# Convolutional self-attention on one core: weights loaded by GpSimd, dummy transposes at the start, the first k loads and the first l and d at other steps, the last group in two blocks and stored by SyncE

## The chip, the cores and the metric

The kernel runs on one core of a Trainium2 chip. The metric is the device time of one execution in microseconds (us), as a median of runs. The engines of the core run side by side, each through its own list of instructions in order, and wait for one another by semaphores: TensorE (PE in the profile, with its weight loads as PEld), VectorE (DVE), ScalarE (ACT), GpSimd (POOL) and SyncE (SP). DMAs are issued from the lists of SP, ACT and POOL and run on 16 DMA engines that they share.

## The reference

For each of four images, with x of 64 x 64 positions and 256 channels:

```python
q = jnp.einsum('bwhc,cd->bwhd', x, Wq) + bq       # 128 channels
k = jnp.einsum('bwhc,cd->bwhd', x, Wk) + bk       # 128 channels
v = jnp.einsum('bwhc,cd->bwhd', x, Wv) + bv       # 256 channels
pq = q.reshape(B, -1, N)                          # N = 4096
pk = k.reshape(B, -1, N)
pv = v.reshape(B, -1, N)
energy = jnp.einsum('bcn,bcm->bnm', pq, pk)
attention = jax.nn.softmax(energy, axis=-1)
out = jnp.einsum('bcm,bnm->bcn', pv, attention)
return gamma * out.reshape(B, W, H, C) + x
```

All of it is float32. The reshape cuts the memory of an image into rows of 4096, whatever the channel a number came from.

## The kernel before, in words

**Numbers in parts.** PE is fed with a rounded 32-bit type. Each factor of the two large products is therefore split into a head and remainders (`halved`, line 244, for q and k; `project_v`, line 262, for v; `upper` and `halves`, lines 320 and 325, for the exponentials), and three products of parts take the place of one.

**The projection of an image.** It has 16 steps (`NI`), i = 0 to 15. A step transposes one block of x (256 KB, loaded by SP, line 82) on PE (line 123), ACT evicts it (129), PE multiplies it by the q and k weights (136), and DVE adds the biases (145). POOL stores q as it is (257, two DMAs), ACT and DVE split k (247, 249), and POOL stores the three parts of k (260). PE makes the values of the step before (157); ACT adds the bias and rounds (166, 267) and DVE makes the two remainders (270). q and k pass through DRAM, in the tiles `qd` and `kf`, because they are read back in another order.

**The attention of an image.** It has 16 groups of 256 rows (`NG`), each of 8 units (`NU`): 128 units, u = 0 to 127. A unit works on four blocks of 128 columns. POOL reads k (`load_k`, 287, 768 KB), SP reads q once a group (`load_q`, 276), and ACT and DVE split it (`halve_q`). `energy` makes the scores in two halves (303) and ACT the exponentials x and y (307). DVE joins them (`join`, 317), ACT makes the head h (`upper`, 322), DVE the remainders l and d (`halves`, 328 and 331). `attend` (351) multiplies h, l and d by the values into the accumulators `a0`, `a1` and `bb`, for two blocks j of 128 rows. One more column of the values holds ones, so `a0` and `a1` also sum the exponentials.

**The end of a group.** ACT copies `bb` (361). `whole` saves the sums (368) and adds `a0` and `a1` (371). `finish`, in pieces over later units, takes the reciprocal times gamma (378, 379), scales (381), transposes (389), adds x (393) and stores through POOL (394).

**Order.** Everything in the block of line 192 runs in the order in which it is written: each engine's list is the order of the calls. The stretch of an image around the change is

```python
for i in range(1, NI):
    ...
    pr.transposed(i + 1)
    begin(b, i)            # first loads, scores, join and upper of the image
    project_qk(b, i)
    project_v(b, i - 1)
halves(b, 0)
project_v(b, NI - 1)
for u in range(STEPS):
    ...                    # energy(u + 3), join(u + 2), upper(u + 2), halves(u + 1), attend(u)
```

`begin` (398) loads the first q at step 8 and splits it at step 9, loads the k of units 0, 1 and 2 at steps 8, 9 and 10, makes the scores of units 0, 1 and 2 at steps 10 to 15, and joins units 0 and 1 at steps 12 and 14. Outside the block, before line 191 and after line 468, the framework places the instructions. POOL builds the unit matrix `ident` for the transposes (86).

**Buffers.** The k tiles, x and h of a unit have three buffers each, y, l and d two, as have the banks of the scores and the tiles of raw q and of split k. So x of unit 3 needs d of unit 0 done, which is the last reader of x of unit 0.

**The guard.** The fast path leaves out the subtraction of the maximum in the softmax. At the end the sums are compared with two bounds (474 to 477), the result is spread over partitions by a product (480) and cast to a flag `again` (481). Every engine reads the flag and branches over a general path, which does not run here (488).

Of the kernel before, what the change touches and what calls it, by code (L numbers as in the profile page):

```python
# [20 lines left out]
def kernel(  # L21
# [67 lines left out]
    wqk_sb = const.tile([P, KC, 2 * C2], F32, name="wqk_sb")  # L89
    nc.scalar.dma_start(wqk_sb[:, :, :C2], wq.rearrange("(k p) d -> p k d", p=P))  # L90
    nc.scalar.dma_start(wqk_sb[:, :, C2:], wk.rearrange("(k p) d -> p k d", p=P))
    wv_sb = const.tile([P, KC, C], F32, name="wv_sb")
    nc.scalar.dma_start(wv_sb, wv.rearrange("(k p) e -> p k e", p=P))
    bqk_sb = const.tile([P, 2 * C2], F32, name="bqk_sb")
    nc.scalar.dma_start(bqk_sb[:, :C2], bq.partition_broadcast(P))
    nc.scalar.dma_start(bqk_sb[:, C2:], bk.partition_broadcast(P))
    bv_sb = const.tile([P, KC], F32, name="bv_sb")
    for eh in range(KC):
        nc.scalar.dma_start(bv_sb[:, eh : eh + 1], bv[eh * P : (eh + 1) * P].unsqueeze(1))
    gam = const.tile([P, 1], F32, name="gam")  # L100
    nc.scalar.dma_start(gam, gamma.partition_broadcast(P))

    class Projection:

# [78 lines left out]
    UPPER = 1.0 - 2.0**-13  # L183

    again = const.tile([P, 1], I32, name="again")

    zall = const.tile([P, B * NG, NJ], F32, name="zall")
    bv4_sb = const.tile([P, KC], F32, name="bv4_sb")
    nc.scalar.mul(bv4_sb, bv_sb, 1.0 / E)

    with ExitStack() as fast:
        fast.enter_context(tc.manual_schedule())
# [12 lines left out]
        vl = qkv.tile([P, NM, C + 2], F32R, tag="vl", name="vl")  # L205
        vd = qkv.tile([P, NM, C], F32R, tag="vd", name="vd")
        for t in (vh, vl):
            nc.vector.tensor_copy(t[:, :, C:], ones[:, : 2 * NM].rearrange("p (m t) -> p m t", t=2))

        images, qd, kf, units, loads, now = [], {}, {}, {}, {}, {}  # L210

# [124 lines left out]
        def attend(b, u, j):  # L336
            g, t = divmod(u, NU)
            if t == j == 0:
                now["acc"] = [
                    ps_o.tile([P, C + 2], F32, tag=f"a{j}", name=f"a{j}_{b}_{g}")  # L340
                    for j in range(NJ)
                ]
                now["bb"] = ps_o.tile([P, NJ, C], F32, tag="bb", name=f"bb_{b}_{g}")
            h, l, d = units[b, u]
            a, bb = now["acc"][j], now["bb"]
            n = slice(j * P, (j + 1) * P)
            for out_, left, right in ((a, h, vh), (a, l, vl), (bb[:, j, :], d, vd)):
                for i in range(4):
                    m = 2 * t + i // 2 + NI * (i % 2)

                    nc.tensor.matmul(  # L351
                        out_,
                        left[:, i, n],
                        right[:, m, :],
                        start=(t == i == 0 and (left is h or left is d and j == 0)),
                        stop=(t == NU - 1 and i == 3 and left is not h),
                        skip_group_check=True,
                    )
            if t == NU - 1 and j == NJ - 1:
                now["o"] = work.tile([P, NJ, C], F32, tag="o", name=f"o_{b}_{g}")  # L360
                nc.scalar.copy(now["o"], bb)

        def whole(b, g):

            o = now["o"]
            for j in range(NJ):
                a = now["acc"][j]
                nc.vector.tensor_copy(zall[:, b * NG + g, j : j + 1], a[:, C : C + 1])
            for j in range(NJ):
                a = now["acc"][j]  # L370
                nc.vector.scalar_tensor_tensor(
# [2 lines left out]

        def finish(b, g, o, xr):
            yield
            r = work.tile([P, NJ], F32, tag="r", name=f"r_{b}_{g}")
            nc.vector.reciprocal(r, zall[:, b * NG + g, :])
            nc.vector.tensor_tensor(r, r, gam.to_broadcast([P, NJ]), ALU.mult)  # L379
            for j in range(NJ):  # L380
                nc.scalar.activation(  # L381
                    o[:, j, :], o[:, j, :], AF.Identity, scale=r[:, j : j + 1]
# [10 lines left out]
            nc.vector.tensor_tensor(xr, xr, tp, ALU.add)  # L393
            nc.gpsimd.dma_start(ov[b, g], xr)

        def begin(b, i):

            if i == 8:
                load_q(b, 0)
            if i == 9:  # L400
                halve_q(b, 0)
            if 8 <= i <= 10:
                load_k(b, i - 8)
            if i >= 10:
                energy(b, (i - 10) // 2, i % 2)
            if i in (12, 14):
# [6 lines left out]
        for b in range(B):  # L413
# [6 lines left out]
            for i in range(1, NI):  # L420
# [3 lines left out]
                    pr.transposed(i + 1)  # L424
                begin(b, i)
                project_qk(b, i)
                project_v(b, i - 1)
                proceed()
            halves(b, 0)
            project_v(b, NI - 1)  # L430
            for u in range(STEPS):
                g, t = divmod(u, NU)
# [24 lines left out]
                    halve_q(b, ahead // NU + 1)  # L457
                for j in range(NJ):
                    attend(b, u, j)
                if t == NU - 1:  # L460
                    whole(b, g)
                    start(finish(b, g, now["o"], loads.pop((b, "x", g))))
                proceed()
# [2 lines left out]
                project_qk(b + 1, 0)  # L466
            while active:
                proceed()


    zs = const.tile([P, 1], F32, name="zs")
    zf = zall.rearrange("p n j -> p (n j)")
    ok = const.tile([P, B * NG * NJ], F32, name="ok")
    nc.vector.tensor_scalar(ok, zf, Z_LOW, None, ALU.is_ge)
    nc.vector.scalar_tensor_tensor(ok, zf, Z_HIGH, ok, ALU.is_le, ALU.mult)
    nc.vector.tensor_reduce(zs, ok, AX.X, ALU.min)
    nc.vector.tensor_scalar(zs, zs, 0.5, None, ALU.is_lt)
    with tc.tile_pool(name="ps_z", bufs=1, space=PSUM) as ps_z:
        zp = ps_z.tile([P, 1], F32, name="zp")
        nc.tensor.matmul(zp, ones, zs, start=True, stop=True)  # L480
        nc.vector.tensor_copy(again, zp)

    NB = 512
    NG = N // NB
# [132 lines left out]
```

## Time and profile before

| | |
|---|---|
| time, median of 3 runs | 2518.38 us (2517.4 to 2519.71) |
| the profiled execution's own time | 2520.6 us |
| its span | 2518.5 us |
| mean granted PE clock | 0.998 |
| PE busy | 2486.5 us, 99% |
| DVE busy | 2103.0 us, 84% |
| ACT busy | 1806.3 us, 72% |
| POOL busy | 425.3 us, 17% |
| k loads (POOL), 768 KB each | 512, median 4.8 us from issue to landing |
| x loads (SP), 256 KB each | 128, median 3.4 us |
| kf stores (POOL), 384 KB each | 64, median 3.5 us |
| output stores (POOL), 256 KB each | 64, median 2.5 us |

The span is the profiled execution from its first to its last instruction. A row of a timeline begins with the start in the span and the duration; then come the engine, the line of the kernel, the operation, what it writes <- what it reads, shapes, and xN for N instructions merged. In square brackets stands how long the engine was idle before, and behind the arrow what ended that. An engine name with a q, as ACTq, is the engine's issuing side. An end of a PE row is modelled; products that follow one another closely overlap in it.

### The profile page before, as it was taken

The page shows a single profiled execution, that of the slowest core. Times are in us where ns is not written, and L with a number is a line of the kernel's source. Part 1 is how long each engine was busy: PE and PEld are TensorE (multiplying, and loading weights), DVE is VectorE, ACT ScalarE, POOL GpSimd, SP SyncE. Part 2 cuts the span into 40 slices and gives each one's busy share as a digit, 9 for nine tenths or more (in the row PEclk, how much of TensorE's full clock was granted, in tenths as well). Part 3 has the DMA queues.
Part 4 walks back from the last instruction along what each step waited for, and adds up shares of the span by engine and source line. Part 5 has one row for each costly group of instructions (what it writes and reads, how often), then busy time and mean ns, then how long its engine had stood idle before and what let it go on. Part 6 is the DMA issues. An engine that isn't in the chain of part 4 may idle for free.

```text
span 2518.5 us, 49987 instructions
## 1 busy us (share of the span) xinstructions
PE 2486.5 (99%) x19970; PEld 2440.1 (97%) x19970; DVE 2103.0 (84%) x2440; ACT 1806.3 (72%) x3138; POOL 425.3 (17%) x774
## 2 busy tenths in 40 slices
PE   8999999999999999999999999999999999999998
PEld 7999999999899999999989999999998999999998
DVE  5888888888688888888868888888886888888887
ACT  5777777777677777777667777777766777777775
POOL 3211111111411111111041111111114111111110
PEclk9999999999999999999999999999999999999999
DMA  6666666665766666666476666666647666666663
GB/s 220 204 207 206 199 200 194 211 196 156 230 214 190 209 202 201 206 192 203 139 236 210 196 200 208 198 205 197 192 144 243 209 207 192 204 200 206 199 196 101
DMA packets 137967, 498.92 MB, mean 198 GB/s; under 512 B 15872, under 2 KB 57856, under 8 KB 137728
## 3 DMA queue, kind: packets, MB, share of 16 engines
q0 software_dynamic: 92160, 453.03, 57.0%
q1 hardware_dynamic: 44032, 41.96, 5.5%
q8 instruction: 160, 2.62, 0.4%
q10 hardware_dynamic: 1536, 0.66, 0.1%
q14 instruction: 79, 0.65, 0.1%
HBM read 445.25 MB, written 50.33 MB: 197 GB/s over the span
## 4 chain that ended last, share of the span: by engine, by line
PE 91%; issue 3%; ACT 3%; DVE 2%; DMA 1%; POOL 0%; POOLq 0%; ACTq 0%; DVEq 0%
PE a L351 38%; PE bb L351 19%; PE sa L303 18%; PE sb L303 10%; PE qk L136 2%; PE v L157 2%; PE ot L389 1%; ACT v L166 1%; DMA k<-kf 1%; ACT vh L267 1%; DVE qks L145 1%; PE xt L123 0%; ACT f L247 0%; DVE vd L270 0%; DVE x L317 0%
## 5 line engine op out<-in xcount | busy, mean ns | idle before, releaser
L307 ACT ACTIVATE x<-sa 128x512 f32<-128x512 f32 x1024 | 608.8, 595 | 431.3 <-PE sa L303 422.3
L317 DVE TENSOR_TENSOR x<-x,y 128x1024 f32<-128x1024 f32 x512 | 625.1, 1221 | 165.6 <-ACT y L307 165.6
L303 PE MATMUL sa<-q,k 128*128 128x256 f32 x4096 | 744.8, 280 | 8.8 <-DMA k<-kf 4.8
L351 PE MATMUL a<-vh,h 128*128 128x258 f32 x4096 | 666.8, 285 | 0.0
L351 PE MATMUL a<-vl,l 128*128 128x258 f32 x4096 | 659.5, 283 | 1.7 <-DVE l L328 1.7
L351 PE MATMUL bb<-vd,d 128*128 128x256 f32 x4096 | 650.7, 281 | 1.8 <-DVE d L331 1.8
L303 PEld LDWEIGHTS sa<-q,k 128*128 128x128 f32 x4096 | 622.9, 188 | 10.8 <-ACT x L307 5.0
L328 DVE TENSOR_TENSOR l<-x,h 128x1024 fp32r<-128x1024 f32 x512 | 623.2, 1217 | 0.0
L331 DVE SCALAR_TENSOR_TENSOR d<-h,x 128x1024 fp32r<-128x1024 f32 x512 | 623.1, 1217 | 0.0
L307 ACT ACTIVATE y<-sb 128x512 f32<-128x512 f32 x1024 | 612.9, 599 | 0.0
L303 PE MATMUL sb<-q,k 128*128 128x256 f32 x2048 | 576.3, 281 | 0.0
L351 PEld LDWEIGHTS a<-vl,l 128*128 128x128 f32 x4096 | 563.0, 189 | 2.6 <-DVE l L328 2.6
L322 ACT ACTIVATE h<-x 128x1024 fp32r<-128x1024 f32 x512 | 543.3, 1061 | 29.1 <-DVE x L317 29.1
L351 PEld LDWEIGHTS a<-vh,h 128*128 128x128 f32 x4096 | 560.6, 190 | 1.1
L351 PEld LDWEIGHTS bb<-vd,d 128*128 128x128 f32 x4096 | 556.4, 188 | 2.6 <-issue 2.0
L287 POOL DMA_DIRECT2D k<-kf x512 | 283.6, 554 | 1487.3 <-PE sb L303 1470.5
L303 PEld LDWEIGHTS sb<-q,k 128*128 128x128 f32 x2048 | 384.5, 188 | 8.9 <-ACT y L307 1.0
L136 PE MATMUL qk<-wqk_sb,xts 128*128 128x256 f32 x512 | 124.5, 387 | 3.5 <-ACT xts L129 3.5
L157 PE MATMUL v<-xts,wv_sb 128*128 128x256 f32 x512 | 120.3, 379 | 0.0
L381 ACT ACTIVATE o<-o,r 128x256 f32<-128x256 f32 x128 | 58.3, 503 | 73.9 <-DVE r L379 73.9
L157 PEld LDWEIGHTS v<-xts,wv_sb 128*128 128x128 f32 x512 | 97.4, 190 | 13.3
L136 PEld LDWEIGHTS qk<-wqk_sb,xts 128*128 128x128 f32 x512 | 94.5, 194 | 14.7 <-ACT xts L129 3.9
(41 smaller groups left out, 876.2 us busy)
## 6 DMA issues: line engine op xcount, KB each, us to landing
k<-kf POOLq DMA_DIRECT2D x512, 768.0 KB, 4.8
x<-in_x_dram SPq DMA_DIRECT2D x128, 256.0 KB, 3.4
kf<-f POOLq DMA_DIRECT2D x64, 384.0 KB, 3.5
out_dram<-x POOLq DMA_DIRECT2D x64, 256.0 KB, 2.5
qd<-qks POOLq DMA_DIRECT2D x128, 64.0 KB, 2.2
qr<-qd SPq DMA_DIRECT2D x64, 128.0 KB, 3.1
wv_sb<-in_L_conv_Wv_dram ACTq DMA_DIRECT2D x1, 256.0 KB, 4.3
wqk_sb<-in_L_conv_Wq_dram ACTq DMA_DIRECT2D x1, 128.0 KB, 2.1
```

The source lines that it names most:

```text
L136: nc.tensor.matmul(qk[:, s, :], self.xt[i][:, k, s, :], wqk_sb[:, k, :], start=(k == 0), stop=(k == KC - 1),)
L145: nc.vector.tensor_tensor(dst, qk[:, :, o : o + w], bqk_sb[:, o : o + w].unsqueeze(1).to_broadcast([P, 2, w]), ALU.add,)
L157: nc.tensor.matmul(vp[:, eh, :], wv_sb[:, k, eh * P : (eh + 1) * P], self.xt[i][:, k].rearrange("p s a -> p (s a)"), start=(k == 0), stop= ...
L287: nc.gpsimd.dma_start(t.rearrange("p (i s) f d -> p i s (f d)", s=2), kf[b, u % NU])
L303: nc.tensor.matmul(to[:, i], kt[:, 2 * k + i, f, :], q[:, :, f, :], start=first, stop=last)
L307: nc.scalar.activation(to[:, 2 * k : 2 * k + 2, :], sp.rearrange("p i j d -> p i (j d)"), AF.Exp, scale=scale,)
L317: nc.vector.tensor_tensor(x, x, y, ALU.mult)
L322: nc.scalar.activation(h, units[b, u], AF.Identity, scale=UPPER)
L328: nc.vector.tensor_tensor(l, x, h.bitcast(F32), ALU.subtract)
L331: nc.vector.scalar_tensor_tensor(d, h.bitcast(F32), 1.0 + E, x, ALU.mult, ALU.subtract)
L351: nc.tensor.matmul(out_, left[:, i, n], right[:, m, :], start=(t == i == 0 and (left is h or left is d and j == 0)), stop=(t == NU - 1 and ...
L381: nc.scalar.activation(o[:, j, :], o[:, j, :], AF.Identity, scale=r[:, j : j + 1])
```

## The change

1. **Weights and biases.** The two biases, Wv, bv and gamma are loaded by DMAs from POOL's list; only Wq and Wk stay in ACT's. The product of bv and 1/E (line 189) moves from ACT to POOL. The columns of ones in the values (208) are copied by ACT and no more by DVE.
2. **Dummy transposes.** Before the block PE transposes `ident` twelve times into a tile that nothing reads.
3. **Steps of the projection.** The first q load moves from step 8 to step 5, the first k loads from steps 8, 9 and 10 to steps 4, 6 and 8. The first l and d (`halves(b, 0)`) move ahead of the values of step 14, made in the last pass of the loop.
4. **The last group** of the last image has a path of its own, `finish_last`, with the guard spread over it: block 0 and block 1 are each scaled by ACT straight from `bb`, added to by DVE from the accumulators, transposed and added to x, and SP stores the group. The other groups are left as they are.

```diff
     wqk_sb = const.tile([P, KC, 2 * C2], F32, name="wqk_sb")
     nc.scalar.dma_start(wqk_sb[:, :, :C2], wq.rearrange("(k p) d -> p k d", p=P))
     nc.scalar.dma_start(wqk_sb[:, :, C2:], wk.rearrange("(k p) d -> p k d", p=P))
+    bqk_sb = const.tile([P, 2 * C2], F32, name="bqk_sb")
+    nc.gpsimd.dma_start(bqk_sb[:, :C2], bq.partition_broadcast(P))
+    nc.gpsimd.dma_start(bqk_sb[:, C2:], bk.partition_broadcast(P))
     wv_sb = const.tile([P, KC, C], F32, name="wv_sb")
-    nc.scalar.dma_start(wv_sb, wv.rearrange("(k p) e -> p k e", p=P))
-    bqk_sb = const.tile([P, 2 * C2], F32, name="bqk_sb")
-    nc.scalar.dma_start(bqk_sb[:, :C2], bq.partition_broadcast(P))
-    nc.scalar.dma_start(bqk_sb[:, C2:], bk.partition_broadcast(P))
+    nc.gpsimd.dma_start(wv_sb, wv.rearrange("(k p) e -> p k e", p=P))
...
-        nc.scalar.dma_start(bv_sb[:, eh : eh + 1], bv[eh * P : (eh + 1) * P].unsqueeze(1))
+        nc.gpsimd.dma_start(bv_sb[:, eh : eh + 1], bv[eh * P : (eh + 1) * P].unsqueeze(1))
...
-    nc.scalar.dma_start(gam, gamma.partition_broadcast(P))
+    nc.gpsimd.dma_start(gam, gamma.partition_broadcast(P))
...
-    nc.scalar.mul(bv4_sb, bv_sb, 1.0 / E)
+    nc.gpsimd.tensor_scalar(bv4_sb, bv_sb, 1.0 / E, None, ALU.mult)
+    with tc.tile_pool(name="ps_w", bufs=1, space=PSUM) as ps_w:
+        wp = ps_w.tile([P, P], F32, name="wp")
+        for _ in range(12):
+            nc.tensor.transpose(wp, ident, ident)
...
-            nc.vector.tensor_copy(t[:, :, C:], ones[:, : 2 * NM].rearrange("p (m t) -> p m t", t=2))
+            nc.scalar.copy(t[:, :, C:], ones[:, : 2 * NM].rearrange("p (m t) -> p m t", t=2))
...
-            if t == NU - 1 and j == NJ - 1:
+            if t == NU - 1 and j == NJ - 1 and (b, g) != (B - 1, NG - 1):
                 now["o"] = work.tile([P, NJ, C], F32, tag="o", name=f"o_{b}_{g}")
                 nc.scalar.copy(now["o"], bb)
...
+        def guard():
+            z = zall.rearrange("p n j -> p (n j)")
+            nc.vector.tensor_scalar(ok, z, Z_LOW, None, ALU.is_ge)
+            nc.vector.scalar_tensor_tensor(ok, z, Z_HIGH, ok, ALU.is_le, ALU.mult)
+            yield
+            nc.vector.tensor_reduce(zs, ok, AX.X, ALU.min)
+            nc.vector.tensor_scalar(zs, zs, 0.5, None, ALU.is_lt)
+            zp = ps_s.tile([P, 1], F32, tag="b", name="zp")
+            nc.tensor.matmul(zp, ones, zs, start=True, stop=True)
+            yield
+            nc.vector.tensor_copy(again, zp)
+            yield
+            yield
+
+        def finish_last(b, g, xr):
+            sums(b, g)
+            r = factors(b, g)
+            check = guard()
+            ra = work.tile([P, NJ], F32, tag="ra", name="ra", bufs=1)
+            nc.vector.tensor_scalar(ra, r, 1.0 + E, None, ALU.mult)
+            o = work.tile([P, NJ, C], F32, tag="o", name=f"o_{b}_{g}")
+            tps = []
+            for j in range(NJ):
+                next(check)
+                nc.scalar.activation(
+                    o[:, j, :], now["bb"][:, j, :], AF.Identity, scale=r[:, j : j + 1]
+                )
+                nc.vector.scalar_tensor_tensor(
+                    o[:, j, :], now["acc"][j][:, :C], ra[:, j : j + 1], o[:, j, :], ALU.mult, ALU.add
+                )
+                tp = (ps_t, ps_s)[j].tile([P, 2, P], F32, tag="ta"[j], name=f"ot_{b}_{g}_{j}")
+                for s in range(2):
+                    nc.tensor.transpose(tp[:, s, :], o[:, j, s * P : (s + 1) * P], ident)
+                tps.append(tp)
+            for j in range(NJ):
+                next(check)
+                n = slice(j * P, (j + 1) * P)
+                nc.vector.tensor_tensor(xr[:, :, n], xr[:, :, n], tps[j], ALU.add)
+            nc.sync.dma_start(ov[b, g], xr)
+
         def begin(b, i):
-            if i == 8:
+            if i == 5:
                 load_q(b, 0)
             if i == 9:
                 halve_q(b, 0)
-            if 8 <= i <= 10:
-                load_k(b, i - 8)
+            if i in (4, 6, 8):
+                load_k(b, i // 2 - 2)
...
                 project_qk(b, i)
+                if i == NI - 1:
+                    halves(b, 0)
                 project_v(b, i - 1)
                 proceed()
-            halves(b, 0)
             project_v(b, NI - 1)
...
-                if t == NU - 1:
+                if (b, u) == (B - 1, STEPS - 1):
+                    finish_last(b, g, loads.pop((b, "x", g)))
+                elif t == NU - 1:
                     whole(b, g)
```

`sums` and `factors` are the saving of the sums and the reciprocal times gamma, cut out of `whole` and `finish` as they were. The guard's lines after the block (471 to 481) are gone.

## The prediction

> **What bounds the kernel now.** I read the page first, then the chain of waits, and then the timeline around every place where TensorE (PE) stood still. The page settles the scale: PE works for almost the whole span, so only its few pauses, and what lies before its first and after its last product, can be won.
>
> ```profile
> span 2518.5 us, 49987 instructions
> PE 2486.5 (99%) x19970; PEld 2440.1 (97%) x19970; DVE 2103.0 (84%) x2440; ACT 1806.3 (72%) x3138; POOL 425.3 (17%) x774
> ```
>
> 2518.5 - 2486.5 leaves 32 us of idle PE, and some busy PE time is slow. There are four places.
>
> The head. In the timeline of the first microseconds (start, duration, engine) PE has transposed two blocks of x by about 6.5 us and then waits, because ACT, which must evict them, waits at line 189 for the last of its own weight transfers and then loads its table:
>
> ```profile
> 4.33 2.19 PE L123 MATMUL xt<-ident,x 128*128 128x128 f32 x8 [4.33 <-DMA x<-in_x_dram]
> 8.02 1.28 ACT L189 ACT_TABLE_LOAD   x1 [8.02 <-DMA gam<-in_L_conv_gamma_dram]
> 9.43 1.05 ACT L129 COPY xts<-xt 128x512 f32<-128x512 f32 x2
> 10.05 3.78 PE L136 MATMUL qk<-wqk_sb,xts 128*128 128x256 f32 x8 [3.52 <-ACT xts L129]
> 14.44 1.89 PE L136 MATMUL qk<-wqk_sb,xts 128*128 128x256 f32 x8
> ```
>
> The last two lines are the same work: 3.78 us on the slow clock, 1.89 us on the full one.
>
> The first scores of an image (step 10). PE waits for k, in image 2 so long that the clock drops again. PE's timeline, then two rows of the stretch view (length, busy PE, PEld, DVE, ACT, POOL, granted clock, DMA):
>
> ```profile
> 1294.44 0.60 PE L123 MATMUL xt<-ident,x 128*128 128x128 f32 x4
> 1297.11 0.47 PE L303 MATMUL sa<-q,k 128*128 128x256 f32 x2 [2.07 <-DMA k<-kf]
> 1297.96 3.50 PE L136 MATMUL qk<-wqk_sb,xts 128*128 128x256 f32 x8
> 1298.00:1302.00 4.00, 4.00 (x13) 3.24 (x13) 0.52 (x2) 1.07 (x2) 0.04 (x1) 0.60 1.05 354
> 1924.00:1928.00 4.00, 4.00 (x23) 3.53 (x22) 1.53 (x4) 1.92 (x5) 1.11 (x3) 1.00 1.10 401
> ```
>
> The first attend of an image. DVE makes l and d of unit 0 behind the values of step 14; ACT's next exp waits for d, the next h for join(2):
>
> ```profile
> 78.87 0.69 DVE L270 SCALAR_TENSOR_TENSOR vl<-vh,v 128x512 fp32r<-128x512 f32 x1 [0.72 <-ACT vh L267]
> 81.36 0.75 PE L351 MATMUL a<-vl,l 128*128 128x258 f32 x4 [0.43 <-DVE l L328]
> 82.53 0.60 ACT L307 ACTIVATE x<-sa 128x512 f32<-128x512 f32 x1 [1.96 <-DVE d L331]
> 84.81 1.06 ACT L322 ACTIVATE h<-x 128x1024 fp32r<-128x1024 f32 x1 [1.19 <-DVE x L317]
> 86.41 0.50 PE L303 MATMUL sa<-q,k 128*128 128x256 f32 x2 [1.00 <-ACT x L307]
> ```
>
> The tail. PE's last product ends at 2506.20; the rest is a chain of small steps, POOL's store and the closing instructions (the last line is one line of the view by source, durations in ns):
>
> ```profile
> 2506.24 0.59 ACT L361 COPY o<-bb 128x512 f32<-128x512 f32 x1 [6.87 <-PE bb L351]
> 2508.05 0.91 ACT L381 ACTIVATE o<-o,r 128x256 f32<-128x256 f32 x2 [1.22 <-DVE r L379]
> 2509.60 0.69 DVE L393 TENSOR_TENSOR x<-x,ot 128x512 f32<-128x512 f32 x1 [1.64 <-PE ot L389]
> 2510.58 0.70 POOL L394 DMA_DIRECT2D out_dram<-x  x1 [26.11 <-DVE x L393]
> L613 POOLq DRAIN  x3: 45/107/6353, 2511.3 to 2518.2; - x3
> ```
>
> The store lands at 2513.82, SP is through its waits at 2514.44, but POOL's 6.35 us drain ends only at 2517.65, and 0.8 us of barriers follow.
>
> **What the Trainium skill says.** "TensorE: Matmul & The Clock Gate", section "What's actually happening": PE's clock is halved until a free-running window of 3413 ns has been busy, and again after an idle one. The trace agrees: at 1297.80 the clock halves for 3.41 us, and from its rise at 14.39 to there are 376 such windows. The 2.07 us wait of image 2 lay wholly in one window; the 1.99 us of image 3 were split by a boundary, and the clock held. The same page, "Part 4: PE-mode transpose", says that transposes do not count as busy PE for this. The trace does not decide: 1.8 us of transposes in the window from 4.15 to 7.56 did not raise the clock, but they filled only half of it. "DMA: Bandwidth & Descriptors", "Specifications": first byte about 1 us from POOL's path, 0.6 us from SP's. POOL's last store shows 1.27 us (2510.58 to 2511.85). "Runtime: NRT & Kernel Launch", "Instruction fetch mechanics": a taken branch outside the fetched pages stalls for a fetch. SP stood 2.55 us after its branch at 2508.43.
>
> **The change part by part.**
>
> Head. ACT keeps two DMA issues, ending at 1.70; the table load of 1.28 us and two small copies (0.32 and 0.19 us on DVE before) end by about 3.6, covered by the wait for x (4.19). The first eviction then waits only for the transposes (done by 5.42) and ends at 5.45 + 0.57 = 6.02; PE leaves the second pair of transposes at 6.31 (5.41 + 4 x 0.21 and the last one's tail). qk starts near 6.35 instead of 10.05: **3.7 us**. wqk landed at 4.55 and stays on ACT. POOL issues six transfers after its mask at 1.31, 0.70 + 5 x 0.54 us as its qd issues take, until about 4.7. The biases should land near 5.5, when qk's end at 8 wants them; wv near 7.5 (before: 6.06), wanted after 8 + 0.4 + 1.7 = 10; bv and gamma near 7.5, then 0.2 us for bv4 on POOL, behind which only the first qd store queues, ready after 8.7. If a transfer came 2 us late it would cost its excess over these 2 us margins.
>
> Clock. Twelve transposes at the slow spacing 0.213 us fill 1.4 to 4.0. Before, the slow clock lasted 4.34 us past 10.05, half of it lost: 2.17 us. If transposes count, almost all of that is won; if not, the wait for a busy window only starts at 6.35 and nothing is. Bounds -1.2 (a bad phase of the window) and +2.2; I take **1.1**.
>
> k. The load of unit 0 moves from step 8 to 4, of unit 1 from 9 to 6, of unit 2 from 10 to 8. From step 10's transposes to the first attend the images take 31.25, 30.30, 34.28 and 32.52 us. Image 1 did not wait, so the others lose 0.95, 3.98 and 2.22: **7.15 us**, of which 1.76 is image 2's slow clock. On POOL a load now stands ahead of the stores of steps 4, 6 and 8, and must wait for the kf stores of units 0, 1, 2. The nearest pair is two steps (7.8 us) apart, a store lands in 3.5. A load occupies POOL for 0.55 us. The 768 KB also run beside x loads (3.4 us to landing, asked for two steps, 7.8 us, ahead). The 128 KB q load moves from 8 to 5 on SP, behind an x load and ahead of one; its qd stores are four steps old. Both are hidden by these margins.
>
> l and d. After the second f (78.15) DVE would do l, d, then four value instructions, and join(2) as before. It saves the gap of 0.72 us and a little: l at 78.08, each large one 1.136 and each small one 0.60 apart, gives join(2) at 78.08 + 2 x 1.136 + 4 x 0.60 = 82.75 instead of 83.56. PE no longer waits for l and d (0.43 + 0.48), but then waits longer for ACT: h of unit 2 follows join(2), x of unit 3 follows h, and the bank follows x. So the gain is not 0.9 + 1.0, but what join(2) gains: 0.8 an image, **3.2 us**. Late next is DVE itself, with the values of steps 14 and 15, first read in units 6 and 7.
>
> Tail. From 2506.20: reciprocal, two small products and the first two guard instructions keep DVE until 2507.07; ACT scales block 0 by 2506.85; DVE adds (0.41) to 2507.51; two transposes to 2508.05. DVE does the guard's reduction and compare, then block 1 at 2508.04 to 2508.45; its transposes end at 2509.0; the copy of the flag (0.14) and two additions of 0.4 end at 2509.48. SP issues the store at 2509.55, 1.03 before POOL did. Then SP still has to issue (0.6), read the flag (0.5), branch with its fetch (2.6) and pass its waits (1.4): done at about 2514.65, with barriers 2515.45. The landing, 3.4 us as the x loads, is inside that. POOL has had nothing to drain since 2484; if its drain is then short, SP ends the kernel: 2518.47 - 2515.45 = **3.0 us**. If it keeps its 6.35 us from about 2509.3, the end is 2516.5: 1.9 us.
>
> Sum: 3.7 + 1.1 + 7.15 + 3.2 + 3.0 = 18.1 us, against the profiled execution's 2520.6 (span 2518.5): 2502.5. The median, 2518.38, lies 2.2 below that execution, and as the window is free-running the 1.76 us of image 2 need not be in it. I take about 17 us off the median: **2501.5 us**.
>
> **The rivals.**
> *Transposes warm nothing and POOL's drain stays.* The page on the clock speaks for the first, nothing for or against the second. 17 - 1.1 - 1.1 leaves 14.8: 2503.6 us. 0.20.
> *The wait moves from k to x.* The k load took 8.3 us in image 2; 768 KB among x loads may make x late. Against it: x has 4.4 us to spare, and step 8 already had such a load beside x. It takes the 7.15 (5.4 where the clock held): about 2507.5 us. 0.10.
> *The new order is not the order that runs, or the weights arrive late.* Outside the hand-ordered block instructions can be placed elsewhere: the guard of before runs ahead of L371. If POOL's transfers land some 4 us later and k gains nothing, some 4 us remain: 2514.5, not to be told from no change (0.2%, 5 us, is about what this measurement can tell). 0.04.
> *Slower: POOL is held by the early k loads.* If a load waits for its kf store to land, the stores queued behind it are late, f's two buffers fill, and ACT and PE stop. At 3.5 us for each of 12 loads that is 42 us, 25 after the gains: 2543 us. It turns the sign from 17 / 12 = 1.4 us a load. The 7.8 us distance speaks against it. 0.03.
>
> **How the numbers follow.** The forecast has 0.63, with 2499 to 2503.5 as its own range. The clock's bounds, the two drains and a half-failed l and d reach 2497 and 2505.5; the x rival reaches 2508. 2497 to 2508 leaves out the last two cases and some edges. Faster 0.93, same 0.04, slower 0.03.
>
> **What would show it.** The first qk near 6.4 us, its eight products 1.9 us long if the clock is up; no PE wait for k in any image, and none of the slow clock; join(2) 0.8 us earlier after the last projection, with PE's wait for ACT's x grown to 1.8 us in place of those for l and d; a short POOL drain and SP last. It is wrong if PE waits at step 10 or for x, if the first value product waits for wv, or if the drain stays at 6 us.

## The result, and the profile after

The changed kernel takes 2520.06 us (median of 6, 2517.64 to 2522.64), the kernel before 2519.62 us in the same rounds (median of 6, 2517.4 to 2521.11): ratio 1.0002, 95% interval 0.9989 to 1.0015. The forecast was 2501.5, its range 2497 to 2508. It is wrong, and the range with it.

The profiled execution took 2518.42 us with a span of 2516.5. The head of the page of the changed kernel:

```profile
span 2516.5 us, 50017 instructions
PE 2497.4 (99%) x19982; PEld 2455.1 (98%) x19982; DVE 2102.5 (84%) x2440; ACT 1806.1 (72%) x3138; POOL 424.6 (17%) x780
```

The span has shrunk by 2.0 us, but PE's busy time has grown by 10.9, from 2486.5 to 2497.4, with 12 instructions more (the head's transposes). So PE stands still 13 us less, and works 11 us longer. The shorter waits were forecast; the longer work was not. PE's largest waits before, from the view of waits of PE (total, times, longest, us):

```profile
PE sa L303 <- DMA k<-kf: 4.8, 3, 2.1
PE xt L123 <- DMA x<-in_x_dram: 4.3, 1, 4.3
PE sa L303 <- ACT x L307: 4.0, 4, 1.1
```

and after:

```profile
PE sa L311 <- ACT x L315: 6.0, 4, 1.6
PE wp L197 <- POOL ident masks.py:199: 2.4, 1, 2.4
PE ot L446 <- DVE o L441: 1.3, 1, 1.3
PE sa L311 <- DVE q L257: 0.3, 1, 0.3
PE xt L123 <- DMA x<-in_x_dram: 0.2, 1, 0.2
```

The waits for k (4.8), for ACT's xts (3.5), for l and d (1.7 and 1.8) and for x (4.3) are gone or nearly so. The one for ACT's x has grown from 1.0 us to 1.3 to 1.6 each time; the working had said that it would grow, to 1.8. A short wait for DVE's q is new. The head, in the timeline of the changed kernel (start, duration, engine):

```profile
2.05 0.32 POOL masks.py:199 TENSOR_SCALAR_AFFINE_SELECT ident<-ident 128x128 f32<-128x128 f32 x1
2.42 2.82 PE L197 MATMUL wp<-ident 128*128 128x128 f32 x12 [2.42 <-POOL ident masks.py:199]
5.30 1.12 PE L123 MATMUL xt<-ident,x 128*128 128x128 f32 x4
6.64 1.12 PE L123 MATMUL xt<-ident,x 128*128 128x128 f32 x4 [0.22 <-DMA x<-in_x_dram]
7.55 2.29 PE L136 MATMUL qk<-wqk_sb,xts 128*128 128x256 f32 x8
10.11 1.89 PE L136 MATMUL qk<-wqk_sb,xts 128*128 128x256 f32 x8
```

The first qk starts at 7.55 in place of 10.05. POOL's first bias load ran ahead of its mask, so the identity was ready a microsecond late, and the twelve transposes held the first x back from 4.33 to 5.30.

The end, in the timeline, with two lines of the view by source (durations in ns):

```profile
2506.17 0.84 ACT L438 ACTIVATE o<-bb,r 128x256 f32<-128x256 f32 x2 [7.09 <-DVE r L380]
2508.16 0.75 DVE L451 TENSOR_TENSOR x<-x,ot 128x256 f32<-128x256 f32 x2
2508.93 0.60 SPq L452 DMA_DIRECT2D out_dram<-x  x1
L661 POOLq DRAIN  x3: 46/107/6683, 2509.0 to 2516.3; - x3
L661 SPq DRAIN  x3: 7/7/13, 2514.5 to 2516.0; - x3
```

The store leaves 1.65 us earlier (1.39, counted from PE's last product), and SP is through at 2514.5; but POOL's drain lasts 6.68 us, no less than before, and ends last.

What takes all of this back is seen in the groups of the page. The scores before:

```profile
L303 PE MATMUL sa<-q,k 128*128 128x256 f32 x4096 | 744.8, 280 | 8.8 <-DMA k<-kf 4.8
L303 PE MATMUL sb<-q,k 128*128 128x256 f32 x2048 | 576.3, 281 | 0.0
```

and after:

```profile
L311 PE MATMUL sa<-q,k 128*128 128x256 f32 x4096 | 759.2, 282 | 6.3 <-ACT x L315 6.0
L311 PE MATMUL sb<-q,k 128*128 128x256 f32 x2048 | 580.4, 283 | 0.0
```

The two groups overlap in time; together the same 4096 and 2048 products keep PE busy 831.8 us in place of 816.9, 14.9 us longer. The attends (L351, now L359) are 2 us shorter together, qk 3.0, and the twelve new transposes add 2.8. The waits before the scores come to 6.3 us, 2.5 less than before. Close up, one half unit of the timeline before (image 1, the scores after the attend of unit 45; start, duration):

```profile
903.29 0.39 PE L303 MATMUL sa<-q,k 128*128 128x256 f32 x2
903.52 0.28 PE L303 MATMUL sb<-q,k 128*128 128x256 f32 x1
903.64 0.39 PE L303 MATMUL sa<-q,k 128*128 128x256 f32 x2
903.86 0.28 PE L303 MATMUL sb<-q,k 128*128 128x256 f32 x1
903.98 0.39 PE L303 MATMUL sa<-q,k 128*128 128x256 f32 x2
```

and after:

```profile
901.73 0.40 PE L311 MATMUL sa<-q,k 128*128 128x256 f32 x2
901.97 0.28 PE L311 MATMUL sb<-q,k 128*128 128x256 f32 x1
902.09 0.40 PE L311 MATMUL sa<-q,k 128*128 128x256 f32 x2
902.32 0.28 PE L311 MATMUL sb<-q,k 128*128 128x256 f32 x1
902.44 0.40 PE L311 MATMUL sa<-q,k 128*128 128x256 f32 x2
```

Six products take 0.69 us before and 0.71 after. In the unrounded starts they are 113 to 114 ns apart before; after, the distances go 117, 120, 116, 115, 119, 116, 120, 117, 115, 118. The whole group of eight units around them, in the stretch view (length, busy PE, PEld, DVE, ACT, POOL, granted clock, DMA), before:

```profile
878.40:913.16 34.76, 34.76 (x294) 34.61 (x293) 30.17 (x34) 25.86 (x44) 5.03 (x9) 1.00 0.65 201
```

and after:

```profile
876.77:911.75 34.98, 34.98 (x294) 34.85 (x293) 30.18 (x34) 25.91 (x44) 4.96 (x9) 1.00 0.65 201
```

PE is busy throughout, at the full clock in both, and takes 0.22 us longer. The balance between the two profiled executions, from the starts of PE's records:

| stretch | before | after | difference | forecast |
|---|---|---|---|---|
| start to image 0's first score | 50.34 | 45.06 | -5.28 | -5.75 |
| first input product to first score, images 1 to 3 | 119.23 | 114.69 | -4.54 | -6.20 |
| first score to first attend of unit 2, four images | 167.32 | 163.62 | -3.70 | -3.2 |
| from there to the image's last product, four images | 2168.48 | 2181.75 | **+13.27** | 0 |
| last product to the end of the span | 12.27 | 10.59 | -1.68 | -3.0 |
| sum | | | -1.93 | -18.15 |

In the third row 1.67 us of the 3.70 are the slow clock window of image 2 before, which the forecast counts with k. Set there, k gained 6.21 us against this one execution, and l and d 2.03.

### The profile page after: what moved, and what is told of

Its sections match the earlier page's. It is cut to its first block, busy times and chain, and to the rows that moved or that the text cites. A ratio compares the mean times of both kernels' runs of the same rounds, so it can differ in the third digit from the quotient of the medians.

```text
span 2516.5 us, 50017 instructions
## 1 busy us (share of the span) xinstructions
PE 2497.4 (99%) x19982; PEld 2455.1 (98%) x19982; DVE 2102.5 (84%) x2440; ACT 1806.1 (72%) x3138; POOL 424.6 (17%) x780
## 4 chain that ended last, share of the span: by engine, by line
## 5 line engine op out<-in xcount | busy, mean ns | idle before, releaser
L311 PE MATMUL sa<-q,k 128*128 128x256 f32 x4096 | 759.2, 282 | 6.3 <-ACT x L315 6.0
L359 PE MATMUL a<-vh,h 128*128 128x258 f32 x4096 | 662.4, 284 | 0.0
L359 PE MATMUL a<-vl,l 128*128 128x258 f32 x4096 | 660.3, 283 | 0.0
L359 PE MATMUL bb<-vd,d 128*128 128x256 f32 x4096 | 651.9, 281 | 0.0
L359 PEld LDWEIGHTS a<-vl,l 128*128 128x128 f32 x4096 | 563.8, 189 | 0.0
L359 PEld LDWEIGHTS a<-vh,h 128*128 128x128 f32 x4096 | 561.5, 189 | 0.0
L359 PEld LDWEIGHTS bb<-vd,d 128*128 128x128 f32 x4096 | 557.6, 189 | 0.0
```

The costliest lines, as they stand in the source:

```text
L311: nc.tensor.matmul(to[:, i], kt[:, 2 * k + i, f, :], q[:, :, f, :], start=first, stop=last)
L359: nc.tensor.matmul(out_, left[:, i, n], right[:, m, :], start=(t == i == 0 and (left is h or left is d and j == 0)), stop=(t == NU - 1 and ...
```

## The experiments

Run n has the label that begins with e and n.

**What could make the same products slower.** Two theories. *Place*: the only new tile in the pool `work` is `ra`, two numbers per partition for the last group's factors. The pool lays out its tiles in the order in which their tags first appear, in steps of 32 bytes. Counted so from the sizes in the code, the tiles that the loop uses keep their places in both kernels, except the two that come after `ra`: `f` and `k` lie 32 bytes further on. k, the stationary operand of the scores (the one that PE holds), lies at 96 bytes modulo 128 of each partition before and at 0 after. q, which streams past it, lies at 32 in both. *Order*: the moved steps change which transfers and evictions run beside the scores all through an image.

Run 1 is the changed kernel with `ra` in r's buffers, which puts k back:

```diff
-            ra = work.tile([P, NJ], F32, tag="ra", name="ra", bufs=1)
+            ra = work.tile([P, NJ], F32, tag="r", name="ra")
```

> The changed kernel, with ra taken from the two buffers of r, so that the tiles of split k (and of f) keep their old addresses (k at 96 modulo 128 instead of 0). Place theory: the attention is slow because these tiles moved by 32 bytes; a group of eight units goes back from 34.99 to about 34.77 us, the products of the scores in units 3 to 7 of a group to 113.3 ns, and the whole to about 13 us below the changed kernel, some 2506 us. Order theory: the earlier l, d and loads set ACT and DVE into another rhythm against PE; nothing changes, about 2519 us.

Run 2 is the kernel before with nothing but a pad ahead of f and k, in the last group (f and k 32 bytes on):

```diff
+            if (b, g) == (B - 1, NG - 1):
+                pad = work.tile([P, NJ], F32, tag="pad", name="pad", bufs=1)
+                nc.gpsimd.memset(pad, 0.0)
```

> The kernel before, with one more tile of 32 bytes at the end of the work pool (set to zero once by POOL in the last group), so that k and f move by 32 bytes as in the changed kernel and nothing else does. Place theory: a group takes 34.99 us, the whole about 13 us more than before, some 2532 us. Order theory: same as before, 34.77 us a group.

Run 3 is the changed kernel with `bufs=2` for `ra`: k another 32 bytes on.

> The changed kernel with two buffers for ra, so that k and f move by another 32 bytes (k at 32 modulo 128). Place theory: if what counts is the place modulo 64 bytes, as fast as with the old addresses, some 2506 us; if it is modulo 128, anything. Order theory: as the changed kernel, about 2519 us.

Run 4 is the kernel before with the moved steps alone:

```diff
-            if i == 8:
+            if i == 5:
                 load_q(b, 0)
...
-            if 8 <= i <= 10:
-                load_k(b, i - 8)
+            if i in (4, 6, 8):
+                load_k(b, i // 2 - 2)
...
+                if i == NI - 1:
+                    halves(b, 0)
                 project_v(b, i - 1)
...
-            halves(b, 0)
             project_v(b, NI - 1)
```

> The kernel before with only the moved steps (first q load at step 5, k loads at 4, 6 and 8, first l and d before the values of step 14); addresses as before. Place theory: the gain that was forecast for these two parts, 7.15 + 3.2 us by the profile and at least 8.5 in a run whose clock held in image 2, so some 2509 us, with 34.77 us a group. Order theory: the loss of some 13 us in the attention comes with it, some 2522 us, with 34.99 us a group.

| run | median us | ratio, 95% interval | eight units, us |
|---|---|---|---|
| 1, ra in r's buffers | 2508.31 | 0.9944, 0.993 to 0.9957 | 34.77 |
| 2, before with k at 0 | 2534.93 | 1.0055, 1.0041 to 1.0069 | 34.97 |
| 3, changed with k at 32 | 2525.97 | 1.002, 1.0013 to 1.0027 | 35.06 |
| 4, moved steps alone | 2513.53 | 0.9971, 0.996 to 0.9983 | 34.77 |

(The ratios stand to the kernel before on the same chip, 2520.88 there; eight units are the median over a profile's groups.) Place it is. Thirty-two bytes in the kernel before cost 14 us, with not one step moved, and the scores' group shows the changed kernel's numbers:

```profile
L303 PE MATMUL sa<-q,k 128*128 128x256 f32 x4096 | 759.2, 282 | 6.2 <-ACT x L307 4.0
```

With thirty-two bytes taken back, the changed kernel goes from the ratio 1.0002 to 0.9944, 12.6 us below the kernel before on that chip, and is faster than both. The order theory falls with run 4: the new order leaves eight units at 34.77. (Its gain falls short of the 2509 expected; the terms below are smaller than forecast too.)

**Is it k's place, or its place against q?** Run 6 moves q and k together by 32 bytes from run 1's places (a pad at the head of `work`), run 9 puts q at 64 but k at 96 modulo 128, where it is fast before, and run 8 puts k at 64 with q at 32 (`bufs=3` for `ra`).

```diff
+        pad = work.tile([P, 8], F32, tag="pad", name="pad", bufs=1)
+        nc.gpsimd.memset(pad, 0.0)
         images, qd, kf, units, loads, now = [], {}, {}, {}, {}, {}
```

> The changed kernel with ra in r's buffers, and both q (32 to 64) and k (96 to 128, that is 0 modulo 128) 32 bytes further on. If the place of k alone decides, the scores are as slow as in the changed kernel: spacing 117.5 ns, 34.98 us for eight units, about 2520 us, ratio 1.000. If the distance from q to k decides, it is still 64 bytes: spacing 113.3 ns, 34.77 us for eight units, about 2507 us, ratio 0.994.

> The changed kernel with three buffers for ra in place of one, so that k lies at 64 modulo 128 (32 bytes after q's place of 32). So far: k at 96 gives score products 113.3 ns apart, at 0 117.5, at 32 118.6. If only the distance of 64 bytes is fast, k at 64 is slow like k at 0, which is as far from q on the other side: 117.5 ns, 34.98 us for eight units, ratio about 1.000. If it is the place alone, anything between 113 and 119 ns is open, and a value below 113 would make a kernel faster than all so far.

> The changed kernel with q at 64 modulo 128 (32 bytes on) and k at 96 modulo 128, the place that it has in the kernel before, so that their distance is 32 bytes as where k lay at 64 beside q at 32. If the distance decides, the scores show that run's repeating spacing of 118, 121, 117, 125, 116, 123 ns, never 113 in a row, about 35.0 us for eight units, ratio 1.000 or a little more. If k's own place decides, 113.3 ns and 34.77 us for eight units, ratio 0.994 to 0.995.

Run 6: 2507.62 us, 0.9951 (0.9937 to 0.9965). Run 8: 2522.83, 1.0006 (1.0 to 1.0013). Run 9: 2523.93, 1.0012 (1.0006 to 1.0019). The stretch of eight units of image 1 in run 6:

```profile
874.19:908.96 34.77, 34.77 (x294) 34.63 (x293) 30.18 (x34) 25.88 (x44) 4.95 (x9) 1.00 0.65 201
```

and in run 9:

```profile
878.61:913.65 35.04, 35.04 (x295) 34.92 (x293) 30.18 (x34) 25.78 (x44) 4.95 (x9) 1.00 0.63 200
```

k at 0 is fast in run 6 and k at 96 slow in run 9; f, which moves with k in every one of these runs, is cleared by run 6 too. Run 9 also shows runs of 118, 121, 117, 125, 116, 123 ns, to a nanosecond or two the rhythm of run 8, which has the same distance. So k's own place does not decide, and its distance from q does.

**Does it hold for the attends, and is the distance enough?** h, l and d lie at 32 modulo 128, as vd does. Run 5 moves them by 64 (and q and k by 128, to keep their places modulo 128); run 11 does the same but moves q and k by 64. Runs 13 and 14 move q and k alone, by 128 and by 64 (run 6 with a wider pad).

```diff
-        vd = qkv.tile([P, NM, C], F32R, tag="vd", name="vd")
+        vd = qkv.tile([P, NM * C + 16], F32R, tag="vd", name="vd")[:, : NM * C]
+        vd = vd.rearrange("p (m c) -> p m c", c=C)
...
-                now["qk"] = work.tile([P, 2, 2 * C2], F32, tag="qk", name=f"qks_{b}_{i}")
+                t = work.tile([P, 4 * C2 + 8], F32, tag="qk", name=f"qks_{b}_{i}")
+                now["qk"] = t[:, : 4 * C2].rearrange("p (s d) -> p s d", s=2)
```

(Run 11 has the first part only.)

> The changed kernel with ra in r's buffers, and besides h, l and d (the stationary operands of the attend products) 64 bytes further on: from 32 to 96 modulo 128, against 32 for the values vh and vd that stream past them. q and k keep their places modulo 128 (32 and 96). If a product is slow because its stationary operand lies at the wrong place against the operand that streams, as k at 0 or 32 beside q at 32, then the attends, now 119 ns apart, are slow for the same reason and would come down towards 113 to 115: 24 of them in a unit and 512 units make 12288 x 5 ns = 60 us, about 2450 us. If the place matters only for the scores, or the attends are slow for the rows of 1032 bytes of vh and vl, nothing changes: 2506 to 2510 us, ratio 0.994.

> As the run in which h, l and d lie 64 bytes further on, but q (96) and k (160, that is 32 modulo 128) moved by 64 and not by 128: the distances stay 64 for scores and for the products with vd, and only the place of q and k against vd differs. If the distances are all that counts, the products with vd stay at 116 ns and the scores are like that run's, mostly 117.8 ns: about 34.79 us for eight units, ratio 0.995 to 0.996. If that run's slow scores came from how the attends before them end, this order may fall into the 113.3 ns spacing: 34.4 us for eight units, 64 x 0.37 = 24 us less, ratio 0.985.

> The changed kernel with ra in r's buffers, q and k both 128 bytes further on (32 and 96 modulo 128, as before), h, l and d where they were. If places count modulo 128, the scores run at 113.3 ns in units 3 to 7 of a group and eight units take 34.77 us as before, ratio 0.994 to 0.995; then it was the move of h, l and d that put the scores of the earlier run at 117.8 ns. If places count over a longer period, 117.8 ns here too, 34.9 us.

> The changed kernel with ra in r's buffers, q and k both 64 bytes further on (96 and 32 modulo 128), h, l and d where they were. If the distance of 64 bytes between q and k is enough for the 113.3 ns rhythm, it shows here as for 32/96 and 64/0: mostly 113.3 ns, 34.75 to 34.8 us for eight units, ratio 0.994 to 0.996. If their own places count as well, 117.8 ns as in the run with h, l and d moved, 34.9 us, ratio 0.998.

Run 5: 2510.66 us, 0.9958 (0.9944 to 0.9971), and not 2450. Run 11: 2516.44, 0.9979 (0.997 to 0.9988), which neither of its two expectations gives. Run 13: 2511.35, 0.996 (0.9945 to 0.9974). Run 14: 2508.97, 0.9955 (0.9938 to 0.9972). All places together. Units are counted here by the attend that runs just before the scores, which are those of four units later. Spacing is the mean distance between the starts of a score product and the next product in units 1 to 7 of the groups after the first scores of an image:

| kernels | q, k mod 128 | k - q mod 128 | spacing, ns | below 115 ns | eight units, us |
|---|---|---|---|---|---|
| before, runs 1, 4 | 32, 96 | 64 | 115.2 | 62-63% | 34.77 |
| run 6 | 64, 0 | 64 | 115.4 | 64% | 34.77 |
| run 14 | 96, 32 | 64 | 115.7 | 59% | 34.80 |
| run 13 | 32, 96 (+128) | 64 | 116.3 | 36% | 34.83 |
| changed, run 2 | 32, 0 | 96 | 117.8 | 0% | 34.98, 34.97 |
| run 3 | 32, 32 | 0 | 119.0 | 2% | 35.06 |
| run 8 | 32, 64 | 32 | 119.4 | 6% | 35.01 |
| run 9 | 64, 96 | 32 | 119.0 | 8% | 35.02 |
| run 5, h, l, d moved | 32, 96 (+128) | 64 | 117.6 | 9% | 34.79 |
| run 11, h, l, d moved | 96, 32 | 64 | 116.7 | 28% | 34.88 |

Every kernel with a share of 10% or more has a distance of 64; no other distance has one. But 64 is not enough: at 64 a unit settles, after its first products, either at 113.3 ns or at about 117.8 (118, 117, 118, 118); before has both, 117.8 in units 1 and 2 of each group and 113.3 in units 3 to 7. Run 5 falls mostly into the slower, run 13 in four units of seven. Run 13 has q and k at the same places modulo 128 as run 1 and yet another mix, so these places alone do not choose. What a unit settles at may hang on how the attends before it end; that isn't shown. Run 5's other half came true: the products with vd, now at a distance of 64 from d, went from 118.2 (run 1) to 116.3 ns; those with vh and vl, whose rows of 1032 bytes shift the place by 8 bytes from row to row, gained 0.6 ns at most. What the attends won, the scores lost. In run 11, with the same 64 between d and vd, the products with vd take 117.7 ns: for them the distance is not shown to be the cause.

**The terms of the forecast.** Run 7 is run 1 without the twelve transposes, run 10 is run 1 with the steps where they were, and run 12 is the kernel before once more.

```diff
-        for _ in range(12):
-            nc.tensor.transpose(wp, ident, ident)
```

> The changed kernel with ra in r's buffers and without the twelve transposes ahead of the first x (they write a tile that nothing reads). If the transposes bring the full clock sooner, as the prediction priced at 1.1 us, the first score starts about 1 us later than with them; if they only delay the first x's own transposes by the microsecond seen in the changed kernel's profile (5.30 in place of 4.33) and the next x is late anyway, nothing moves. Either way the ratio stays within 0.9935 to 0.995, and only the profile's first 20 us can tell.

> The changed kernel with ra in r's buffers and without the moved steps (loads of k and q, l and d of unit 0 where they were): the new head and the new end alone, at the old addresses. By the theory that the parts add and only the place was missed, it gains what the whole (0.9944) gains beyond the moved steps alone (0.9971): 0.27%, about 6 us by the times, though the profiles give only 3 to 4 us at the head and 1.7 at the end; ratio 0.997 to 0.9985. If head and end are worth nothing by themselves, ratio 1.000. Eight units take 34.77 us and PE waits for k again in three images.

> The kernel before, unchanged: a second profile of it. The forecast's terms for the first scores (PE's waits for k, 4.8 us in three images, and one window of slow clock) and for the head (first score product input at 10.05 us) were read from one execution. If they belong to the kernel, this profile shows them again within a few tenths. If the landing of k and x differs from one execution to the next, as the 1.2 us of k waits in the run with head and end alone suggests, the waits differ by some microseconds; ratio 1.000.

Run 7: 2508.73 us, 0.9954 (0.994 to 0.9967). Run 10: 2510.32, 0.9958 (0.9944 to 0.9971), more than expected. Run 12: 2520.05, 0.9999 (0.999 to 1.0008). Its waits of PE:

```profile
PE qk L136 <- ACT xts L129: 5.4, 1, 5.4
PE xt L123 <- DMA x<-in_x_dram: 4.7, 2, 4.1
PE sa L303 <- ACT vh L267: 1.7, 1, 1.7
```

No wait for k by name; but the 1.7 us stand before the first score of image 3, which doesn't read vh. The landings of the transfers settle it. In the four profiles with the old steps (before, runs 2, 10, 12) the first score of an image starts 0.135 or 0.136 us after the k of unit 0 has landed, in 15 of 16 images (image 1 of before is the other). So PE waits for k in nearly every image of the old order, run 12's included, and only the length differs: from its first input product to its first score image 1, 2 and 3 lose 0, 2.31 and 2.23 us before and 0.22, 0.51 and 1.98 in run 12. With the new steps k has landed more than 12 us ahead in all 48 images. The mechanism is the kernel's; the 4.8 us and the slow window of image 2 were one execution's.

Taking all profiles, four with the old order of steps (before, runs 2, 10, 12) and twelve with the new, gives each term its size:

- *Head.* Image 0's first score starts at 50.34, 51.96, 51.90 and 51.27 in the four with the old head (before, runs 12, 2 and 4), and at 45.06 to 48.82, mean 47.28, in the twelve with the new: 4.1 us, image 0's wait for k included. The old wait ends with ACT's table load, which started at 8.02, 10.34, 10.97 and 10.19, and the copies behind it; in the new head it ends with x, whose second block was transposed between 6.6 and 8.4. (In run 4, with the old head, that block came at 8.53.) Without the twelve transposes the first score starts at 48.13, inside the spread of the others, so one run doesn't show what they are worth.
- *k.* From an image's first input product to its first score the new order takes 38.23 us in images 1 to 3, in every profile. The old takes 4.54, 2.71, 3.00 and 1.92 us more over the three (before, runs 12, 2 and 10); before and run 2 also lose 1.67 to a slow window after it. Mean 3.0 + 0.8.
- *l and d.* From first score to the first attend of unit 2 the old order takes 41.40 to 41.48 where the clock holds, the new 40.50 to 40.66 in 21 of its 48 images: the 0.8 us of the working. In 14 others the clock is halved in that stretch, which then takes 42.0 us or more: 1.7 us over four images. In the remaining 13, nine of them an image 2, and in two of the 14, the scores run up to 1.0 us late: 0.8 us over four images. There the third score product starts 0.054 to 0.056 us after DVE has written the second remainder of the first q, so PE waits for the split of q, the next thing that the earlier scores run into. In the changed kernel's image 1 (timeline of PE and of DVE):

```profile
669.65 0.36 PE L311 MATMUL sa<-q,k 128*128 128x256 f32 x1
670.30 0.39 PE L311 MATMUL sa<-q,k 128*128 128x256 f32 x1 [0.29 <-DVE q L257]
669.83 0.75 DVE L257 SCALAR_TENSOR_TENSOR q<-q,qr 128x256 fp32r<-128x256 f32 x2
```

  Raw q has landed 20 us or more before; ACT and DVE come to the split without a pause, behind their other work. The mean of the new order is 41.24, so 0.7 us are left of 3.2.
- *End.* 12.27 us from the last product to the end in the old, 12.57 in run 2; 10.59 to 10.61 in all the new: 1.7 us. POOL's drain is 6.353 us in all four of the old and 6.683 in all twelve of the new.

The slow window after the moved l and d, in the timeline of run 1 (image 0):

```profile
83.81 0.50 PE L311 MATMUL sa<-q,k 128*128 128x256 f32 x2 [1.61 <-ACT x L315]
85.36 1.04 PE L359 MATMUL a<-vl,l 128*128 128x258 f32 x4
88.77 0.64 PE L359 MATMUL bb<-vd,d 128*128 128x256 f32 x4
```

and in its stretch view (granted clock in the column after POOL):

```profile
86.00:88.00 2.00, 2.00 (x11) 2.00 (x11) 2.00 (x3) 1.65 (x3) 0.00 (x0) 0.50 0.65 123
```

PE idles 1.61 us for ACT's x, and at 85.36 the clock falls to half for one window of 3.41 us, which costs 1.46. With the old wait of 1.0 us it happened in none of 16 images. What tells the 14 from the other 34 of the new order is where the window falls. Counted from the clock's rise in steps of 3.413 us, all 14 waits (1.27 to 1.64 us) lie in one window and begin in its first 1.27 us. Three more begin so early and last 1.23 to 1.44 us without effect. Of the 31 that begin later in a window none halved the clock.

Together 4.1 + 3.8 + 0.7 + 1.7 = 10.3 us. Between profiles that is right: spans of 2507.3 (run 1) and 2517.4 (mean of before and run 12), 10.2 apart; run 10, 5.8 by its terms, is 6.8 lower. The timed ratios give a little more (run 1 at least 0.43%, 10.8 us; run 10 at least 0.29%, 7.3 us). The profiled execution is the slowest of five in both runs; beyond that no term here explains it.

## Why the prediction was wrong

**The step that failed** is one that the working does not have. The sum sets the gains "against the profiled execution's 2520.6" and so leaves every other product at its old speed: it puts the change in the attention loop at nothing. The tile `ra` was counted as one small product on DVE (it takes 0.17 us); that it takes 32 bytes in front of k has no place in the working. It costs 13.3 us of the profiled execution, and runs 1 and 2 show it by itself from both sides: 12.6 us below the kernel before without it, and 14 us above with nothing else. None of the rivals had it. The slower one had its mechanism in POOL's queue; among PE's waits in the changed kernel the only one for POOL is that for its mask, at the start. That the loss and the gains cancel to 1.0002 is chance.

The terms that were mis-sized, taking the profiles together:

- *Head 3.7 and clock 1.1, with 0.95 for image 0's k*: measured 4.1 in place of 5.75. ACT's part is right; the mask behind a POOL transfer and x's own lateness took the rest. On the clock, the working left open whether transposes count, and the first rival rests on their not counting. The Trainium skill ("TensorE: Matmul & The Clock Gate", "Part 4: PE-mode transpose") was quoted as saying that transposes don't count as busy PE. In run 14 the clock rises at 5.84, 2.3 us before the first product of the kernel that isn't a transpose (8.17); the window behind it, 2.43 to 5.84, holds PE's transposes alone:

```profile
2.42 2.82 PE L197 MATMUL wp<-ident 128*128 128x128 f32 x12 [2.42 <-POOL ident masks.py:199]
5.30 0.90 PE L123 MATMUL xt<-ident,x 128*128 128x128 f32 x4
7.68 0.66 PE L123 MATMUL xt<-ident,x 128*128 128x128 f32 x4 [1.49 <-DMA x<-in_x_dram]
8.17 1.03 PE L136 MATMUL qk<-wqk_sb,xts 128*128 128x256 f32 x4
```

  In run 11 too the clock rises, at 6.37, before the first other product (8.88). So transposes count here. (The trace calls them MATMUL, as every product; whether they ran in the mode that the page has in mind isn't shown.) Whether they help in an execution depends on where the window falls: the clock rose between 5.84 and 14.23 in the eleven heads that have them (in run 11 it was lost again at 9.78, after the wait for x, and back at 13.19), at 13.40 in the one that has not.
- *k 7.15*, or 6.2 without image 0's share: 3.8, and the mechanism right: with the new steps the first score waits for k in no image of any run. The size was read from one execution that lost more than the others; the note that image 2's slow window "need not be in it" went in the right direction, not far enough. Nor did the wait move to x, as a rival had it: PE waits for x in the head alone, in every profile. It moved in part to the split of q, which the working does not look at; of q it follows the load alone.
- *l and d 3.2*, measured 0.7: the step was right to 0.1 us and the wait grew to 1.6 where 1.8 was forecast; but the same working had quoted a 2.07 us wait that halved the clock and one of 1.99 that didn't, and did not ask what 1.6 us would do. 29% of the images pay 1.46 us for it. The working has the clock halved after an idle window. No window before a halving was idle: in the 17 of all profiles, the fall at each kernel's end left out, PE is busy for 1.34 to 2.11 of the 3.41 us, 1.34 in the one before 1297.80.
- *End 3.0*: 1.7. The other value that the working gave, 1.9 with the drain unchanged, is the one that came. POOL drained 6.68 us though its last transfer was issued at 2483.55, 25 us earlier, and 6.35 us right behind a store: the drain is not the longer for a store just issued.

## What to carry to other kernels

Compare the addresses of the tiles that PE reads, before and after an edit: a tile of eight bytes, allocated in a pool ahead of an operand, can cost or win half a per cent with no wait to show for it; the sign is PE's busy time growing at full clock with the same count of products. The size of a wait in one execution is not yet the kernel's: over four profiles the k term is 3.8 and not 6.2. And a longer single wait of PE can cost more than its length: here waits of some 1.6 us cost another 1.46 in 14 of 48 images, those of 1.0 us never.

## What was not expected of the hardware

- The spacing of 128x256 fp32 products hangs on the places of the stationary and the streaming operand in the partition: 113.3 ns in a steady run is seen for long only with the two 64 bytes apart modulo 128; otherwise repeating patterns with means of 117.8 (96 apart), 119.0 (0) and 119.0 to 119.4 (32). The Trainium skill ("TensorE: Matmul & The Clock Gate", "Step-by-step: what each phase is for") says that PE reads the two through independent ports, and that loading the next weights takes nothing from the running product. No run here measures the bandwidth. The spacing does depend on how the two lie: a 32-byte shift of one against the other takes its mean from 115.2 to between 117.8 and 119.4 ns, 2 to 4%.
- At 64 bytes two steady spacings exist, 113.3 and 117.8 ns, for the same operands. What chooses between them, and why the places matter at all, stays open.
- A wait of 1.2 to 1.6 us halves the clock for 3.41 us in 14 of 48 cases, and which ones hangs on where in the window it begins; a wait of 1.0 us in 0 of 16.
- Transposes alone raised the clock (runs 14 and 11).
- With the old steps the first three k loads of an image, 768 KB each, landed after 5.8 to 8.5 us, from one image and execution to the next.
